# Two graph layers on one core: the products with counts in three passes, x in pieces, and layer 2's first operands fetched early

## The chip, the cores and the metric

The kernel runs on one core of one Trainium2 chip. The metric is the device time in microseconds of one execution on that core. A core has TensorE (PE, with its weight loads shown apart as PEld), VectorE (DVE), ScalarE (ACT), GpSimd (POOL) and SyncE (SP). Each engine takes its own instructions in the order in which they were written down; SP, ACT and POOL also issue DMAs in that order.

## The reference

A two-layer graph network (GIN) on 6250 nodes and 100000 edges, followed by a residual sum and a layer norm:

```
agg(h) = (1 + eps) * h + segment_sum(h[src], dst)
h1  = relu(relu(agg1(x) @ W1a + b1a) @ W1b + b1b)      # 256 -> 512 -> 512
y   = relu(agg2(h1) @ W2a + b2a) @ W2b + b2b           # 512 -> 512 -> 256
out = layernorm(x + y)
```

`x` is 6250 x 256 in float32. The edges are sorted by `dst`, and `dst` is 6250 times the square of a uniform number, so the first nodes have many edges and the last ones few: the first 768 nodes have about a third of all edges.

## The kernel before, in words

Nodes are taken in 49 tiles of 128, edges in 782 chunks of 128. The first tiles (six in layer 1, five in layer 2, the "heavy" ones, `HEAVY`) are summed in another way than the rest.

**Light nodes.** Chunks are taken in groups of four or more (`order`). For each chunk POOL issues one indirect DMA (L277) that gathers the 128 source rows into the buffer `early` (in layer 2 `early` and `late`); the buffers hold 24 chunks. PE adds the rows by slot with a 0/1 matrix (L1143), ACT copies the result (L1162), PE puts the slots in place (L1174), and DVE adds the result to the accumulators `acc` of the tiles concerned (L1166). Accumulators are seeded by a DMA on SP with the nodes' own rows (`seed`).

**Heavy nodes, layer 1.** For 264 chunks no rows are gathered. `counting` makes two 0/1 matrices for a chunk on DVE (`ca` at L965, `cb` at L968), PE multiplies them (L1011), ACT copies the sum (L1020) and DVE adds it into `at` (L981), a matrix of counts of source by destination in SBUF, that has room for four destination tiles (`RING`) at a time. It runs from the last chunk down, in 157 steps: the first 104 hold one chunk, then come 36 of two, 12 of four and 5 of eight. `turned_products` then multiplies: for each of 13 ranges of four source tiles (`RANGE`) it loads x (`load`), cuts it into three bf16 pieces whose sum is x (`pieces_of`, `thirds`: two casts on ACT, two subtractions on DVE), copies the counts to `ci` on ACT (L992), writes them to DRAM for layer 2 (`counts`), and PE multiplies pieces with counts (L917). This is done in two passes: tiles 4 and 5 (256 columns) while counting goes on, between steps 47 and 100, and tiles 0 to 3 (512 columns) after all counting. Each pass loads and cuts all of x.

**Heavy nodes, layer 2.** `products` loads each range of h1 and cuts it, loads the counts of one tile and range at a time (L864), and PE multiplies (L881) into one bank per tile and range; DVE adds that to `acc`.

**Dense part.** `block` takes two finished tiles: transposes (L772), the first product (L794), ReLU on ACT (L798), the second product (L808), and `finish`. Layer 1 writes h1 to DRAM from ACT's queue; layer 2 makes the layer norm and writes the output.

**Order.** All engines' instructions are written in one order (`manual_schedule`). After every chunk the program writes down one step of the dense blocks (`blockwise`, two blocks at a time) and as many steps of the heavy work (`beside`) as a credit allows. The credit per chunk (`spread`) is worked out from the estimated work of each kind; a step that costs nothing ends the turn. What evacuates a PSUM bank is written down 7 chunks later (`LAG`). At the end of a layer the rest is written out without gathers. Layer 2's gathers need all of h1, and before its first group six steps of `beside` are written.

Of the kernel before, what the change touches and what calls it, by code (L numbers as in the profile page):

```python
# [17 lines left out]
P = 128  # L18
# [134 lines left out]
def tile_gin_residual_layernorm(  # L153
# [359 lines left out]
    def weight(pool, w, kk, width, name):  # L513
        t = pool.tile([P, kk, width], F32, name=name)
        (nc.scalar if pool is const else nc.sync).dma_start(t, w.rearrange("(k p) f -> p k f", p=P))
        return t

    def second(pool):
        t = pool.tile([P, D], F32, name="b2b_s")
        nc.sync.dma_start(t, b2b.partition_broadcast(P))  # L520
        return weight(pool, w2a, KH, H, "w2a_s"), weight(pool, w2b, KH, D, "w2b_s"), t

    w1a_s = weight(const, w1a, KD, H, "w1a_s")
    w1b_s = weight(const, w1b, KH, H, "w1b_s")
# [39 lines left out]
    def ordered(ctx):  # L564
# [7 lines left out]
        counts = odram.tile([len(ranges), HEAVY[1], P, RANGE * P], F16, name="counts")  # L572

        def layer(number, ctx, table, width, scale, wa, ba, wb, wide, prepare, finish, conclude):
# [243 lines left out]
            UNIT = RANGE if number == 1 else RANGE // 2  # L818

            def load(r):  # L820

                units = []
                for u in range(0, len(ranges[r]), UNIT):
                    ks = ranges[r][u : u + UNIT]
                    xr = dense.tile([P, UNIT, width], F32, tag="xr", name="xr", bufs=2 if once else 3)
# [11 lines left out]
            def pieces_of(units):  # L837

                found = {}
                for ks, n, xr in units:  # L840
                    xp = dense.tile(
                        [P, 3, UNIT, width], BF16, tag="xp", name="xp", bufs=2 * RANGE // UNIT
                    )
                    if n:
                        thirds([xp[:, i, :n, :] for i in range(3)], xr[:, :n, :])
                    if n < len(ks):
                        m = rows(ks[n])
                        thirds([xp[:m, i, n, :] for i in range(3)], xr[:m, n, :])
                    for j, k in enumerate(ks):
                        found[k] = xp[: rows(k), :, j, :]  # L850
                return found

            def products():

                turns = [(r, t) for r in range(len(ranges)) for t in heavy]
                loaded, cut, factors = {}, {}, []

                def fetch(i):
                    r, t = turns[i]
# [649 lines left out]
```

## Time and profile before

| what | us |
|---|---|
| median of three runs | 1761.97 (1754.29 to 1763.14) |
| the profiled execution: its time | 1546.14 |
| the profiled execution: its span | 1544.2 |
| PE busy | 1315.8 (85%) |
| POOL busy | 1061.0 (69%) |
| DVE busy | 824.4 (53%) |
| ACT busy | 492.3 (32%) |

All durations are those of the profiled execution; its time and the median of the runs stand 216 us apart. The mean granted PE clock in it is 0.928. An engine's matmuls overlap and their ends are modelled, so a busy PE is not a PE at its peak; what one matmul takes is read from the starts of matmuls that follow each other. "issue" as a releaser means that the engine waited for nothing that the profile shows.

### The profile page before, as it was taken

How to read it: one execution, taken by the hardware profiler on the slowest of the kernel's cores; microseconds unless marked ns; L12 is line 12 of the kernel's file. 1: busy time of each engine (PE TensorE's matmuls, PEld its weight loads, DVE VectorE, ACT ScalarE, POOL GpSimd, SP SyncE). 2: the span in 40 equal slices, each digit the busy share in tenths (PEclk: the TensorE clock that was granted, in tenths of full speed). 3: DMA queues.
4: the chain of work that ended last, by engine and by line, in shares of the span. 5: the costliest groups of instructions: out<-in, count | busy, mean ns of one | idle time of the engine just before them, and what ended most of it. 6: DMA issues, size and time to landing. Idle time of an engine off the chain costs nothing.

```text
span 1544.2 us, 19261 instructions
## 1 busy us (share of the span) xinstructions
PE 1315.8 (85%) x6399; PEld 679.5 (44%) x6399; DVE 824.4 (53%) x2112; ACT 492.3 (32%) x897; POOL 1061.0 (69%) x1070
## 2 busy tenths in 40 slices
PE   2557778878888999999957798999999999999997
PEld 1114444434433444455522242444445655555556
DVE  7986666587763444333124335454545455556553
ACT  0455454342323444323332122222222222333131
POOL 6777777777777756773057777777777777777720
PEclk8668889998998999999978899999999999999999
DMA  5535654444435666543378888878888888888731
GB/s 144 155 98 147 183 174 147 131 134 126 135 115 170 193 185 205 149 136 97 105 243 284 271 282 259 280 245 282 257 281 260 259 260 248 261 265 251 236 115 34
DMA packets 144516, 301.14 MB, mean 195 GB/s; under 512 B 24430, under 2 KB 73242, under 8 KB 144408
## 3 DMA queue, kind: packets, MB, share of 16 engines
q0 software_dynamic: 67904, 209.00, 44.5%
q1 hardware_dynamic: 67196, 76.18, 15.1%
q10 hardware_dynamic: 9308, 14.64, 2.7%
q8 instruction: 54, 0.88, 0.2%
q14 instruction: 54, 0.44, 0.1%
HBM read 272.50 MB, written 27.23 MB: 194 GB/s over the span
## 4 chain that ended last, share of the span: by engine, by line
PE 55%; DMA 13%; DVE 12%; POOL 8%; issue 6%; ACT 5%; DVEq 1%; SPq 0%; ACTq 0%; POOLq 0%
PE bank L808 14%; PE bank L794 14%; PE bank L1143 8%; PE bank L1174 7%; PE bank L881 5%; POOL early L277 5%; PE bank L917 4%; DMA xr<-in_x_dram 3%; DMA early<-h,srcs 3%; POOL late L277 3%; DVE acc L1166 2%; DMA acc<-h 2%; DMA late<-h,srcs 2%; PE bank L1011 1%; PE bank L772 1%
## 5 line engine op out<-in xcount | busy, mean ns | idle before, releaser
L277 POOL DMA_INDIRECT early<-in_x_dram,srcs x518 | 525.7, 1015 | 184.7 <-issue 136.8
L277 POOL DMA_INDIRECT early<-h,srcs x274 | 267.5, 976 | 153.4 <-DMA h<-h1r 70.3
L1166 DVE SCALAR_TENSOR_TENSOR acc<-bank,mask,acc 128x256 f32<-128x256 f32 (+1 forms) x426 | 238.6, 608 | 232.3 <-PE bank L1174 178.9
L277 POOL DMA_INDIRECT late<-h,srcs x264 | 265.3, 1005 | 80.4 <-issue 64.0
L1143 PE MATMUL bank<-early,sel 128*32 128x256 f32 (+1 forms) x1584 | 167.1, 496 | 58.3 <-DMA early<-in_x_dram,srcs 32.8
L881 PE MATMUL bank<-xp,ci 128*128 128x512 bf16 (+1 forms) x735 | 177.7, 392 | 17.6 <-DMA ci<-counts 14.3
L794 PE MATMUL bank<-zt,w2a_s 128*128 128x256 f32 (+2 forms) x832 | 178.8, 369 | 4.9 <-ACT split L1162 2.0
L808 PE MATMUL bank<-w1b_s,ht 128*128 128x512 f32 (+1 forms) x392 | 180.8, 607 | 0.8 <-ACT ht L798 0.5
L1174 PE MATMUL bank<-split,to 128*128 128x256 f32 (+3 forms) x368 | 176.5, 563 | 3.1 <-DVE acc L1166 1.5
L794 PEld LDWEIGHTS bank<-zt,w2a_s 128*128 128x128 f32 x832 | 151.0, 191 | 43.4 <-issue 15.4
L881 PEld LDWEIGHTS <-ci 128*128 128x128 f16 (+1 forms) x735 | 71.7, 100 | 132.3 <-issue 62.8
L1162 ACT COPY split<-bank 128x256 f32<-128x256 f32 (+3 forms) x184 | 87.9, 483 | 130.1 <-PE bank L1143 101.1
L1011 PE MATMUL bank<-cb,ca 128*128 128x490 f16 x264 | 91.8, 416 | 43.7 <-DVE cb L968 14.5
L917 PE MATMUL bank<-ci,xp 128*128 128x256 f16 (+2 forms) x588 | 119.1, 348 | 5.9 <-ACT ci L992 5.9
L543 DVE TENSOR_TENSOR xr<-xr,xp 128x1024 f32<-128x1024 f32 (+2 forms) x51 | 60.2, 1181 | 106.9 <-ACT xp L542 95.7
L794 PE MATMUL bank<-zt,w1a_s 128*128 128x256 f32 (+1 forms) x400 | 102.4, 397 | 13.3 <-DVE acc L1166 5.6
L808 PEld LDWEIGHTS bank<-w1b_s,ht 128*128 128x128 f32 (+1 forms) x392 | 75.5, 196 | 85.1 <-issue 74.9
L1174 PEld LDWEIGHTS bank<-split,to 128*128 128x128 f32 (+1 forms) x368 | 58.1, 197 | 122.3 <-issue 76.2
L965 DVE TENSOR_SCALAR ca<-numbers,low 128x128 f16<-128x128 f16 x264 | 69.5, 263 | 72.1 <-PE bank L1011 71.7
L798 ACT ACTIVATE ht<-bank,b2a_s 128x256 f32<-128x256 f32 (+2 forms) x104 | 42.7, 460 | 183.7 <-PE bank L794 163.8
L1143 PEld LDWEIGHTS bank<-early,sel 128*32 128x32 f32 x1584 | 33.9, 112 | 149.2 <-issue 106.4
L1020 ACT CAST cs<-bank 128x490 f16<-128x490 f32 x157 | 85.6, 579 | 40.2 <-DVE at L981 28.1
(129 smaller groups left out, 1396.8 us busy)
## 6 DMA issues: line engine op xcount, KB each, us to landing
xr<-in_x_dram SPq DMA_DIRECT2D x24, 512.0 KB
h<-h1r ACTq DMA_DIRECT2D x48, 256.0 KB
xr<-h SPq DMA_DIRECT2D x24, 512.0 KB
acc<-h SPq DMA_DIRECT2D x23, 512.0 KB
early<-in_x_dram,srcs POOLq DMA_INDIRECT x518
ci<-counts SPq DMA_DIRECT2D x60, 128.0 KB
acc<-in_x_dram SPq DMA_DIRECT2D x24, 256.0 KB
counts<-ci SPq DMA_DIRECT2D x12, 512.0 KB
```

The costliest lines, as they stand in the source:

```text
L277: nc.gpsimd.indirect_dma_start(out=rows_[:, j, :], out_offset=None, in_=table, in_offset=bass.IndirectOffsetOnAxis(ap=srcs[:, c : c + 1], ...
L794: nc.tensor.matmul(ph[0][:, :nb], wa[:, k, f * P : (f + 1) * P], zt[:, k, :nb], start=(k == 0), stop=(k == kk - 1),)
L808: nc.tensor.matmul(po[0][:m], ht[:, f, i * P : i * P + m], wb[:, f, :], start=(f == 0), stop=(f == KH - 1),)
L881: nc.tensor.matmul(pm[0], ci[: rows(k), j * P : (j + 1) * P], cut[r][k][:, h, :], start=(j == 0 and h == 0), stop=(j == len(ks) - 1 and h ...
L917: nc.tensor.matmul(sums[f][0].rearrange("p (t c) -> p t c", c=P), cut[r][k][:, h, f * P : (f + 1) * P], factors[r][: rows(k), : len(ts), j ...
L965: nc.vector.tensor_scalar(a, numbers[:, :P], low[:, c : c + 1], None, op0=ALU.is_equal)
L1011: mm = nc.tensor.matmul(pc[0], a, b, start=(i == 0), stop=(i == n - 1))
L1020: nc.scalar.copy(cs, ap)
L1143: mm = nc.tensor.matmul(pm[0][b * SLOTS : (b + 1) * SLOTS], sel[:, c - c0, :], rows_[:, j, :], start=(c == parts[b][0]), stop=(c == parts[ ...
L1162: nc.scalar.copy(split[:used], ap[:used])
L1166: nc.vector.scalar_tensor_tensor(acc[t], ap, mask[:, t - lo[g], g : g + 1], acc[t], op0=ALU.mult, op1=ALU.add,)
L1174: nc.tensor.matmul(pu[0], to[:used], split[:used], start=True, stop=True)
```

## The change

- Layer 1 makes three passes of two tiles each (256 columns): tiles 4 and 5 as before; tiles 2 and 3 while the counting of tiles 0 and 1 goes on (from step 108, the products dealt over the steps after ten more); tiles 0 and 1 after all counting. The sums of a pass lie in one PSUM bank.
- Only the first pass loads and cuts x. It writes the pieces to DRAM (`x_cut`), and the other two load pieces from there, two ranges ahead. The last pass multiplies with `at` itself, without the copy `ci`.
- The counts for layer 2 go to DRAM as one tensor per range (`kept`), and layer 2 loads a range's counts in one DMA.
- The factor `ca` is made for four chunks in one DVE instruction.
- `at` and layer 2's rows, pieces and counts share one piece of SBUF (`room`). At the end of layer 1, when the heavy work is done and at most four groups are left, SP loads two ranges of h1 and one range of counts, and the first range is cut. Layer 2 takes ranges 2 to 12 first, then 0 and 1, and writes ten steps of `beside` before its first group. h1 is cut one tile at a time.
- `w1a_s` and `w1b_s` are no longer constants: they lie in a pool of layer 1, and layer 2's weights take their place.

```diff
+        kept = odram.tile([len(ranges), P, RANGE, LATE], F16, name="kept")
+        x_cut = odram.tile([len(ranges), P, 3, RANGE, D], BF16, name="x_cut")
...
+        line = [r for r in range(len(ranges)) if ranges[r][0] >= HEAVY[0]]
+        line += [r for r in range(len(ranges)) if r not in line]
...
             def products():
-                fetch(0)
                 yield 0.0
+                for i, t in [(i, t) for i in range(len(line)) for t in heavy]:
+                    r = line[i]
+                    if t == heavy[0]:
+                        fetch_counts(i + 1)
+                        fetch_rows(i + 2)
+                    if t == heavy[min(1, tiles - 1)]:
+                        cut_pair(i + 1, 0)
+                    if t == heavy[min(3, tiles - 1)]:
+                        cut_pair(i + 1, 1)
+                    ci = counts_of[i]
...
-            def turned_products(ts, factor):
+            def turned_products(ts, again, factor):
...
+                def come(r):
+                    if r < len(ranges):
+                        if again:
+                            xp = dense.tile(
+                                [P, 3, RANGE, width], BF16, tag="xp", name="xp", bufs=3
+                            )
+                            moved(r, xp, False)
+                            coming[r] = xp
+                        else:
+                            coming[r] = load(r)
 
                 def ready(r):
                     if r < len(ranges):
-                        cut[r] = pieces_of(loaded.pop(r))
+                        xp = coming.pop(r)
+                        if not again:
+                            xp = pieces_of(xp)
+                            moved(r, xp, True)
+                        found[r] = xp
                         factors[r] = factor(r, ts)
 
+                come(0)
+                come(1)
                 yield 0.0
                 ready(0)
-                sums = [place(n) for _ in range(kk)]
+                sums = place(kk * n, whole=True)
...
                         if j == len(ks) // 2:
                             ready(r + 1)
+                            come(r + 2)
...
-                        nc.vector.tensor_scalar(
-                            a, numbers[:, :P], low[:, c : c + 1], None, op0=ALU.is_equal
-                        )
+                            nc.vector.tensor_tensor(
+                                a, numbers[:, :P].unsqueeze(1).to_broadcast([P, AHEAD, P]),
+                                low[:, c0 : c0 + AHEAD].unsqueeze(2).to_broadcast([P, AHEAD, P]),
+                                op=ALU.is_equal,
+                            )
...
+                passes = [heavy[i : i + 2] for i in range(0, tiles, 2)][::-1]
+                for i, ts in enumerate(passes):
+                    first = END[ts[0]] + 1
+                    yield from advance(first)
+                    product = products_of(ts, i > 0)
+                    if ts[0] == RING:
+                        yield from along(product, apart)
+                        while cleared < len(ranges):
+                            yield 0.0
+                    elif ts[0] > RING:
+                        yield from product
+                    else:
+                        yield from along(product, len(STEPS))
...
             if number == 2:
-                for _ in range(6):
+                for _ in range(10):
                     beside.step()
...
+                if k >= len(order) - 4 and ahead and not beside.todo:
+                    ahead.pop(0)()
...
         with ExitStack() as inner:
-            layer(1, inner, x, D, e1[:, 0:1], w1a_s, b1a_s, w1b_s, H, prepare1, finish1, conclude1)
+            w1a_s, w1b_s = first_two(inner.enter_context(tc.tile_pool(name="first", bufs=1)))
+            ahead = [
+                lambda: (fetch_rows(0), fetch_counts(0)), lambda: fetch_rows(1),
+                lambda: None, lambda: cut_pair(0, 0), lambda: cut_pair(0, 1),
+            ]
```

`along(product, upto)` takes the counting steps up to `upto` and, after the first ten, deals the product's steps evenly among them. `fetch_rows` and `fetch_counts` issue SP's loads into `room`; `cut_pair` cuts two tiles of a range.

## The prediction

> **What bounds the kernel now.** I first cut the span by engine and stage. The columns are the stretch in us, its length, busy time of PE, of PE's weight loads, of DVE, ACT and POOL (with instruction counts), the granted PE clock, the DMA share and GB/s.
>
> ```profile
> 192.00:330.00 138.00, 114.44 (x596) 60.46 (x595) 93.31 (x283) 62.15 (x121) 105.74 (x106) 0.91 0.50 149
> 330.00:475.00 145.00, 116.82 (x566) 57.24 (x568) 98.69 (x336) 42.40 (x97) 111.48 (x111) 0.94 0.43 128
> 475.00:640.00 165.00, 152.44 (x697) 72.93 (x690) 64.94 (x113) 71.84 (x102) 111.95 (x111) 0.93 0.61 188
> 640.00:713.00 73.00, 69.99 (x340) 38.41 (x340) 31.29 (x75) 24.95 (x60) 55.56 (x58) 1.00 0.46 139
> 713.00:777.00 64.00, 59.84 (x211) 32.98 (x209) 13.69 (x27) 18.18 (x44) 0.69 (x1) 1.00 0.26 93
> 777.00:810.00 33.00, 18.73 (x76) 6.94 (x80) 8.62 (x7) 10.26 (x11) 20.27 (x20) 0.69 0.72 246
> ...
> 1220.00:1480.00 260.00, 249.67 (x1227) 149.98 (x1220) 143.14 (x307) 71.30 (x149) 197.22 (x207) 0.99 0.81 254
> ```
>
> POOL issues the gathers, one instruction each. It takes 145/111 = 1.31 us per gather while counting runs (330 to 475), 165/111 = 1.49 in 475 to 640, and 73/58 = 1.26 after that. So POOL paces layer 1 up to 475, something slows it from 475 to 640, and from 713 to 777 PE works alone. The waits by stretch (waiter, releaser, us in total, times, longest) tell what: the first line is from 330 to 475, the second from 475 to 640, the third from 640 to 777.
>
> ```profile
> PE bank L1143 <- DMA early<-in_x_dram,srcs: 14.4, 9, 2.9
> ...
> POOL early L277 <- PE bank L1143: 19.6, 9, 4.9
> ...
> POOL early L277 <- PE bank L1143: 3.1, 2, 2.8
> ```
>
> Before 475 PE waits for gathered rows and has 28 us idle. After it POOL waits for PE, 22.7 us in all. That is just where the products for four node tiles run: all 294 matmuls of 512 columns at L917 lie between 478 and 639. The timeline shows their pace (first line) and that of 256 columns (second), and then one dense block near the end of layer 1.
>
> ```profile
> 528.20 2.75 PE L917 MATMUL bank<-ci,xp 128*128 128x512 f16 x12
> ...
> 158.30 0.82 PE L917 MATMUL bank<-ci,xp 128*128 128x256 f16 x6
> ...
> 740.00 7.03 PE L808 MATMUL bank<-w1b_s,ht 128*128 128x512 f32 x16
> 746.87 3.62 PE L794 MATMUL bank<-zt,w1a_s 128*128 128x256 f32 x16
> ```
>
> Start to start, six of 256 take 0.66 us (the next instruction starts at 158.96), 0.110 each; the chain of waits gives twelve of 512 as 2.59 us, 0.216 each. A dense block of two tiles is 7.03 + 3.62 + 0.60 of transposes = 11.2 us of PE. At the layers' border:
>
> ```profile
> 783.95 0.94 POOL L277 DMA_INDIRECT early<-h,srcs  x1 [70.26 <-DMA h<-h1r]
> ...
> 789.34 0.58 PE L881 MATMUL bank<-xp,ci 128*128 128x512 bf16 x1 [14.30 <-DMA ci<-counts]
> ...
> 808.37 2.78 PE L1143 MATMUL bank<-early,sel 128*32 128x512 f32 x24
> ```
>
> POOL restarts only when the last row of h1 has landed. PE loses 15 us at its first products, and reaches the first group 25 us after POOL's restart, inside the 24 gathers that the buffers hold (24 x 1.29 = 31 us). POOL then issues 538 gathers by 1480.3, in 696 us, 1.29 each: it paces layer 2, followed by PE alone to 1544.
>
> **What the Trainium skill says.** "TensorE: Matmul & The Clock Gate", Back-to-back issue gap, gives 262 cycles for 256 columns and 518 for 512 at 2.4 GHz: 109 and 216 ns. The trace agrees (110 and 216), so narrower products cost nothing but their count. "SBUF — State Buffer", Who interferes with whom, says that a tensor_scalar in a two-port mode locks GpSimd out of the port it writes descriptors through, while tensor_tensor takes only reads. The trace agrees in sign: a gather's busy time is 1.004 us where counting runs, 0.958 where it has ended. "VectorE: DVE Perf Modes", The perf-mode tier table, gives tensor_tensor at most 2x on 16-bit data. "DMA: Bandwidth & Descriptors", Specifications, puts full rate at runs of 512 B or more; no wait in this trace shows short runs costing anything.
>
> **The change, part by part.**
> (1) Passes. Matmul work goes from 294 x 0.110 + 294 x 0.216 = 95.8 us to 882 x 0.110 = 97.0: +1.2 us. What counts is the place. Pass two (tiles 2 and 3) starts after counting step 108 + 10 and is dealt evenly over the 39 steps left; 22 of those hold two chunks, 12 four, 5 eight, so 56% of it falls on the first 44 of 132 chunks, which now run from about 285 us. Its 32.3 us thus go mostly where PE waited for POOL. The side queue's credit per gathered chunk is unchanged and so is its estimated work, so counting ends later, near 525 on the old clock, and pass three ends near the old 640. From 475 to 640 PE then has pass three (32.3), about a fifth of pass two (6) and some 40 chunks of counting (40 x 0.21 = 8.4), 47 in place of 63.5. PE's 152 falls to some 136, below POOL's 111 x 1.31 = 145. The stretch becomes POOL's: 165 to 145, of which I take **18** (bounds 8 and 22.7, the waits themselves).
> (2) PE's lag. POOL's last gather of layer 1 is issued at 712.7, PE's last gather sum starts at 724.4. With some 3 us to land, 8 are lag from the stretch before: take **7** (0 to 8).
> (3) The dense block of tiles 2 and 3 becomes ready near 535 instead of with tiles 0 and 1 after 640. The tail from 724 to 775 is 4.5 such blocks in a row; one goes from it: **11** (5 to 22). It lands in 535 to 640, in the room between PE's 136 and POOL's 145.
> (4) x pieces. The second cutting goes: 12 x (1.22 + 1.26) = 29.8 us of DVE, 12 x 2.09 = 25.1 of ACT. In cuts of 512 columns the first costs 24 x 2 x 0.68 = 32.6 of DVE (+2.8) and 24 x 2 x 0.59 = 28.2 of ACT (+3.1). ACT's copies of counts fall from 12 x (1.89 + 1.04) to 24 x 1.04, and pass three has none. For that SP issues 12 writes and 24 reads of 768 KB (27.6 MB) where 12 reads of 512 KB (6.3) were; the DMA share is 0.43 to 0.61 here, and the 21 MB are 0.05 of a share over 300 us. On SP a write waits for DVE's third piece; behind it stand the next load, the counts' write and seeds of accumulators, which are each issued one to two ranges early. Zero, covered by that lead. The first read of a pass has no lead: 768 KB at 1.5 times the old 5 to 6 us stands PE still for 8 to 9 us. Pass three replaces the old start (478.5 to 489.8, load, cut and copy); pass two's is new, covered by POOL's full buffers, +8 if they are not full.
> (5) First factors in fours: 264 x 0.263 = 69.5 us of DVE become 66 instructions of 128x512. Nearest row: the f32 is_equal of 128x512 at 0.683; at the tier table's 2x, an estimate, 0.41. So 27 to 45 us, and no longer two-port. Of the 0.046 us that a gather is longer, over some 300 gathers, 42% (69.5 of 69.5 + 95.4) is 6 us: take **3** (0 to 6).
> (6) Counts in one tensor per range: the same bytes, runs of 256 and 512 B written and 5 KB read. Zero; reads are off PE's path, being a range ahead. Layer 2's cuts per tile add 48 x 2 x 0.68 - 59.6 = 5.7 us of DVE and 6 of ACT, engines that idle half of that stage: zero.
> (7) Border. Two ranges and their counts are in SBUF, and the first range's pieces are cut, before the last h1 lands; their memory is last read by pass three, 100 us before. PE does five products at once and four more when the second range is cut. But w2a and w2b now take the memory of w1a and w1b, so SP holds their loads, and the accumulator seeds behind them, until the last L808 of layer 1 (they went at 762 to 764). Seeds, scaling and the second cut then end near 25 us after it, and PE gets to the first group 33 to 37 us after layer 1's last matmul; it was 33. POOL, which restarts 9 us after, blocks at about 40. Zero, and a few us of loss if that is missed. What is gained is 4 x 12 x 0.216 = 10.4 us of products done in PE's idle time. From 1220 to 1480 PE is busy 249.7 of 260 with no wait for rows, so part of that comes back at the end: **4** (-5 to 10).
> Sum: 18 + 7 + 11 + 3 + 4 - 1 = **42 us** off the profiled execution (span 1544.2, time 1546.1): 1504. The runs' median is 1762, 216 us above; no view shows where those lie. I carry the difference over unscaled: **1720**. Were every stage stretched alike, it would be 48 and 1714.
>
> **Rivals.**
> *POOL paces more than I think.* If the stretch to 640 is POOL's in the timed runs already (1056 gathers that took 0.2 us longer would make up the 216), items 1 and 2 are worth little and 3 with some of 7 remains: 15 us, 1747. For it: POOL's even pace; against it: its 22.7 us of waits on PE.
> *Late pieces: slower.* SP is one queue. A pass needs 13 loads; in pass three a range lasts about 6 us and the load is issued 1.5 ranges ahead, 9 us, against an estimated 7.5 to 10.8 us for 768 KB (1.5 times the 5.0 to 7.2 of the chain's xr loads), with seeds ahead of it in the queue. PE waits in order, the gather sums behind it, then POOL. From 42/26 = 1.6 us per load in both passes the gain is gone; at 2.5 it is +23, 1785. Against it: the old load had half a range of lead and a cut behind it, and cost 13 us in all.
> *Pass two overfills PE before 475.* PE's idle there is partly waiting for DVE's second factors, which more matmuls don't shorten. If 30 of the 32 us show as POOL waits, 10 us remain: 1755, no change.
> *The fetch comes too late to help*: item 7 falls to 0, 1724; inside my own range.
>
> **How the numbers follow.** Mine has 0.60, own range 1693 (69 off, all upper bounds) to 1749 (13 off). POOL's pace 0.15, overfilled 0.08, late pieces 0.17. Within 0.5% is 9 us, about what a measurement of this kernel can tell. Faster 0.75, same 0.08, slower 0.17. The range 1690 to 1770 leaves out most of the slow case and a few per cent below.
>
> **What would show it.** Right: no POOL wait on PE beyond 10 us from 285 to 640; layer 1's last gather near 690; four or fewer dense blocks after it; POOL's first gather from h1 at 740 to 750, and 696 us to its last; PE busy at the border. Wrong: PE waiting for the DMA of the pieces, POOL waiting on PE between 285 and 475, or the first group of layer 2 more than 40 us after the last L808. A tail of layer 1 still above 50 us breaks item 3.

## The result and the profile after

| kernel | median, us | lowest to highest |
|---|---|---|
| before | 1758.13 | 1753.57 to 1763.14 |
| after | 1778.11 | 1776.95 to 1782.20 |

The ratio is 1.0117, 95% interval 1.0078 to 1.0156: 20 us slower, where 42 us faster was forecast.

One thing has to be known before any trace is read. **The chips are of two sorts.** The kernel before takes 1754 to 1773 us on one sort and 1544 to 1546 us on the other. The profile that the prediction was made from (1546 us) is of the second sort, the runs shown beside it are of the first; for that profile this is told from its time and its trace alone. Each of the six chips of the later runs was used in one group only, so the chip and its state at that hour can't be told apart. So I compare only kernels run on the same chip, or traces of the same sort; "the slower sort" and "the faster sort" below mean this. The kernel after, run again on a chip of the faster sort, took 1557.42 us against 1546.35 (ratio 1.0060, 1.0035 to 1.0085). It is slower on both, so the chips don't excuse the forecast.

What differs between the sorts is read from the busy line (engine, us, share of the span, instructions) of the page of the kernel before on the slower sort, and of the kernel after on both, slower first:

```profile
PE 1397.1 (79%) x6369; PEld 700.3 (40%) x6399; DVE 830.6 (47%) x2112; ACT 492.0 (28%) x897; POOL 1063.4 (60%) x1070
```

```profile
PE 1407.4 (79%) x6693; PEld 728.3 (41%) x6693; DVE 805.5 (45%) x1960; ACT 467.4 (26%) x942; POOL 1035.2 (58%) x1070
```

```profile
PE 1317.2 (84%) x6661; PEld 708.0 (45%) x6693; DVE 803.7 (51%) x1960; ACT 467.3 (30%) x942; POOL 1037.8 (66%) x1070
```

DVE, ACT and POOL are busy for the same time on both sorts (DVE 824.4, ACT 492.3 and POOL 1061.0 in the profile before, against 830.6, 492.0 and 1063.4). So the instructions of these three are as fast, and what they lose lies between the instructions. PE's busy time, whose ends are modelled, is 81 to 90 us longer. What the change saves in work is there too: DVE 824 to 804, ACT 492 to 467.

The windows that answer to those of before, for the same gathers and on the same sort of chip (kernel after; us, busy us and instructions of PE, PEld, DVE, ACT, POOL, then clock, DMA share, GB/s):

```profile
182.00:349.00 167.00, 126.00 (x665) 68.57 (x665) 100.06 (x248) 70.87 (x140) 106.28 (x106) 0.87 0.57 177
349.00:493.00 144.00, 133.36 (x794) 75.58 (x792) 86.75 (x229) 52.29 (x108) 110.39 (x111) 0.99 0.63 196
493.00:638.00 145.00, 132.57 (x798) 80.41 (x796) 55.89 (x143) 33.16 (x80) 107.56 (x111) 0.96 0.70 224
638.00:711.00 73.00, 70.34 (x316) 36.99 (x316) 25.53 (x61) 21.30 (x53) 54.23 (x58) 1.00 0.54 171
711.00:778.00 67.00, 61.16 (x231) 33.42 (x232) 20.49 (x38) 22.64 (x51) 0.93 (x1) 1.00 0.19 63
778.00:810.00 32.00, 21.60 (x78) 8.11 (x78) 14.14 (x25) 11.99 (x19) 19.23 (x20) 0.79 0.85 318
1222.00:1488.00 266.00, 254.80 (x1257) 150.81 (x1257) 148.98 (x317) 77.03 (x159) 197.39 (x205) 0.99 0.80 246
```

Read against before, row by row: 138 us have become 167, 145 are 144, 165 are 145, 73 are 73, 64 are 67, 33 are 32, 260 are 266. The third row has the size that the prediction promised, 165 to 145 us, with PE busy 133 and POOL's pace of 1.31 us per gather; whether the third pass is the reason is asked below. In the second row, where pass two was put, PE is busy 133 us in place of 117 and the stretch is no longer. The first row ate the gain and more: 29 us for the same 106 gathers, with PE busy 126 of 167.

The following table has the whole kernel in that manner: us between the starts of POOL's gathers (L277), numbered from 0 to 1055; 517 is the last of layer 1, 518 the first of layer 2. "Both repairs" is a kernel of mine that is told of below. The columns are the traces before, f2, i1, b1 and after.

| gathers | before, faster sort | after | both repairs | before, slower sort | after |
|---|---|---|---|---|---|
| 0 to 111 | 150.4 | 144.5 | 146.1 | 174.4 | 166.9 |
| 111 to 185 (pass one) | 100.2 | 116.6 | 107.4 | 115.6 | 131.7 |
| 185 to 230 (its end) | 57.9 | 67.9 | 64.0 | 71.2 | 68.6 |
| 230 to 370 (pass two begins) | 184.0 | 184.3 | 184.3 | 205.4 | 209.5 |
| 370 to 444 | 114.8 | 93.0 | 94.0 | 128.5 | 120.3 |
| 444 to 517 | 96.1 | 96.9 | 93.4 | 110.7 | 112.1 |
| 517 to 518 (border) | 71.2 | 74.0 | 69.3 | 79.7 | 85.6 |
| 518 to 830 | 411.6 | 408.3 | 406.1 | 460.7 | 459.5 |
| 830 to 860 | 37.6 | 48.5 | 48.5 | 45.5 | 52.1 |
| 860 to 1055 | 246.2 | 246.7 | 246.7 | 290.5 | 286.2 |
| from 1055 to the end | 64.8 | 73.3 | 64.3 | 74.7 | 75.8 |

Single executions of one kernel lie up to 1% apart, so a row is believed when several kernels agree on it. Three losses pass that test, named here with the faster sort first: gathers 111 to 230, in which pass one lies (+26 and +13 us); the border, from the last gather of layer 1 to the first of layer 2 (+3 and +6); and gathers 830 to 860 (+11 and +7).

**Pass one.** The waits of the kernel before (faster sort, gathers 111 to 240; waiter, releaser, us in total, times, longest), and then those of the kernel after:

```profile
ACT acc L641 <- DMA acc<-in_x_dram: 6.9, 2, 4.2
ACT xp L542 <- DMA xr<-in_x_dram: 6.6, 3, 3.0
...
POOL early L277 <- PE bank L1143: 0.6, 2, 0.3
```

```profile
ACT xp L548 <- DMA xr<-in_x_dram: 26.7, 6, 6.4
POOL early L277 <- PE bank L1251: 26.5, 10, 9.1
...
ACT acc L709 <- DMA acc<-in_x_dram: 22.3, 3, 7.6
```

ACT stood 13.5 us for rows of x and for seeds before, and stands 49 us after. The chain goes on: the copies of the gathers' sums (`split`) stand behind that on ACT, PE waits for them, and POOL's wait on PE grows from 0.6 to 26.5 us, as much as the stretch is longer. In the kernel with both repairs it is 10.4 us:

```profile
POOL early L277 <- PE bank L1258: 10.4, 7, 4.7
```

**The border.** DMA issues of SP and ACT around the last store of h1, and POOL's first gather of layer 2, kernel after, faster sort (start, us, queue and line):

```profile
771.94 0.43 SPq L515 DMA_DIRECT2D w2a_s<-in_L_gnn_W2a_dram  x1
772.41 0.51 SPq L515 DMA_DIRECT2D w2b_s<-in_L_gnn_W2b_dram  x1
784.05 1.39 SPq L702 DMA_DIRECT2D acc<-h  x3
```

```profile
772.93 0.48 ACTq L1311 DMA_DIRECT2D h<-h1r  x1
```

```profile
784.98 1.00 POOL L277 DMA_INDIRECT early<-h,srcs  x1 [73.05 <-PE bank L934]
```

And SP and ACT in the kernel before:

```profile
762.69 0.43 SPq L515 DMA_DIRECT2D w2a_s<-in_L_gnn_W2a_dram  x1
763.16 0.51 SPq L515 DMA_DIRECT2D w2b_s<-in_L_gnn_W2b_dram  x1
763.71 2.11 SPq L634 DMA_DIRECT2D acc<-h  x3
```

```profile
776.46 0.48 ACTq L1199 DMA_DIRECT2D h<-h1r  x1
```

Before, w2's 1.5 MB were issued 14 us ahead of the last store (776.5). After, they wait for w1's memory and go out in the very microsecond ahead of it. From that store's issue to layer 2's first gather it took 7.5 us before, on both sorts, and 12.1 (faster) and 11.9 (slower) after. The DMA packets in the traces say how. On the slower sort the weights' queue moves 1.3 MB in the 4 us after 892.7, at some 330 GB/s, and the store's first packet comes 5.1 us after its issue (at 895.9), where it came 0.8 us after it before the change. From its first packet to the end of its last it then takes 5.5 us, against 5.4: the store isn't slowed, it starts later. POOL's gather follows the last packet by 1.3 us in both kernels, so it waits for the store, though the line above names PE, which gave the last signal.

What the early fetch was for did come true. The first products of layer 2 follow layer 1's last matmul without a pause, and then PE waits:

```profile
772.29 13.11 PE L934 MATMUL bank<-room 128*128 128x512 bf16 x58 [0.78 <-DVE h1r L1309]
792.90 3.67 PE L934 MATMUL bank<-room 128*128 128x512 bf16 x7 [7.50 <-DMA room<-kept]
...
810.93 1.50 PE L1251 MATMUL bank<-early,sel 128*32 128x512 f32 x12
```

The first group comes 25.9 us after POOL's restart; it was 24.4.

**Pace and blocks** have not changed. Six matmuls of 256 columns, and a dense block near the end of layer 1 (kernel after, faster sort):

```profile
562.50 0.82 PE L996 MATMUL bank<-room,xp 128*128 128x256 f16 x6
...
748.02 7.03 PE L876 MATMUL bank<-w1b_s,ht 128*128 128x512 f32 x16
754.89 3.62 PE L862 MATMUL bank<-zt,w1a_s 128*128 128x256 f32 x16
```

### The profile page after: what moved, and what is told of

It reads as the page before. It is cut to its first block, busy times and chain, and to the rows that moved or that the text cites. A ratio compares the mean times of both kernels' runs of the same rounds, so it can differ in the third digit from the quotient of the medians.

```text
span 1776.1 us, 19688 instructions
## 1 busy us (share of the span) xinstructions
PE 1407.4 (79%) x6693; PEld 728.3 (41%) x6693; DVE 805.5 (45%) x1960; ACT 467.4 (26%) x942; POOL 1035.2 (58%) x1070
## 4 chain that ended last, share of the span: by engine, by line
PE 48%; issue 17%; DVE 9%; another core or an unknown queue 8%; DMA 8%; ACT 4%; POOL 3%; SPq 1%; DVEq 1%; ACTq 0%; POOLq 0%
PE bank L862 11%; PE bank L876 10%; PE bank L1251 8%; PE bank L934 7%; PE bank L1282 5%; PE bank L996 3%; DMA acc<-h 3%; DMA xr<-in_x_dram 2%; PE bank L1075 2%; POOL early L277 2%; POOL late L277 1%; PE bank L840 1%; DVE acc L1274 1%; DVE room L1065 1%
## 5 line engine op out<-in xcount | busy, mean ns | idle before, releaser
L277 POOL DMA_INDIRECT early<-in_x_dram,srcs x518 | 514.4, 993 | 300.3 <-issue 133.9
L277 POOL DMA_INDIRECT early<-h,srcs x274 | 263.3, 961 | 224.0 <-PE bank L934 90.0
L1274 DVE SCALAR_TENSOR_TENSOR acc<-bank,mask,acc 128x256 f32<-128x256 f32 (+1 forms) x426 | 239.6, 609 | 256.2 <-PE bank L1282 73.7
L277 POOL DMA_INDIRECT late<-h,srcs x264 | 255.0, 966 | 141.2 <-issue 71.3
L1251 PE MATMUL bank<-early,sel 128*32 128x256 f32 (+1 forms) x1584 | 192.2, 535 | 68.9 <-ACT split L1270 35.6
L862 PE MATMUL bank<-zt,w2a_s 128*128 128x256 f32 (+2 forms) x832 | 192.5, 379 | 30.8 <-issue 23.2
L934 PE MATMUL bank<-room 128*128 128x512 bf16 (+1 forms) x735 | 185.4, 400 | 37.5 <-issue 17.6
L1282 PE MATMUL bank<-split,to 128*128 128x256 f32 (+3 forms) x368 | 184.3, 586 | 12.8 <-issue 6.9
L876 PE MATMUL bank<-w1b_s,ht 128*128 128x512 f32 (+1 forms) x392 | 183.5, 615 | 7.4 <-ACT ht L866 3.2
L1052 DVE TENSOR_SCALAR cb<-numbers,spot 128x490 f16<-128x490 f16 x264 | 90.0, 354 | 164.5 <-PE bank L1075 74.4
L934 PEld LDWEIGHTS <-room 128*128 128x128 f16 (+1 forms) x735 | 72.2, 101 | 154.1 <-issue 79.3
L996 PEld LDWEIGHTS <-xp 128*128 128x128 bf16 x882 | 91.7, 105 | 67.5 <-issue 44.1
L876 PEld LDWEIGHTS bank<-w1b_s,ht 128*128 128x128 f32 (+1 forms) x392 | 76.0, 198 | 92.1 <-issue 81.3
L1251 PE MATMUL bank<-late,sel 128*32 128x512 f32 x528 | 90.3, 651 | 27.2 <-issue 14.3
L996 PE MATMUL bank<-ci,xp 128*128 128x256 f16 (+1 forms) x588 | 91.7, 300 | 16.5 <-ACT ci L1109 11.3
L940 DVE TENSOR_TENSOR acc<-bank,acc 128x512 f32<-128x512 f32 x65 | 43.5, 683 | 132.8 <-remote 73.7
```

Source lines behind the costliest of these rows:

```text
L277: nc.gpsimd.indirect_dma_start(out=rows_[:, j, :], out_offset=None, in_=table, in_offset=bass.IndirectOffsetOnAxis(ap=srcs[:, c : c + 1], ...
L862: nc.tensor.matmul(ph[0][:, :nb], wa[:, k, f * P : (f + 1) * P], zt[:, k, :nb], start=(k == 0), stop=(k == kk - 1),)
L876: nc.tensor.matmul(po[0][:m], ht[:, f, i * P : i * P + m], wb[:, f, :], start=(f == 0), stop=(f == KH - 1),)
L934: nc.tensor.matmul(pm[0], ci[: rows(k), j, t * P : (t + 1) * P], cut[k][:, h, :], start=(j == 0 and h == 0), stop=(j == len(ks) - 1 and h ...
L940: nc.vector.tensor_tensor(acc[t], ap, acc[t], op=ALU.add)
L996: nc.tensor.matmul(sums[0][:, f * n : (f + 1) * n], found[r][:m, h, j, f * P : (f + 1) * P], factors[r][:m, j, :], start=(k == 0 and h == ...
```

## The experiments

My theory: the three passes give what the prediction said or less, and single new waits on SP's queue and on the DMAs take it away. The first rival: the schedule itself is at fault. Kernels in one group without another remark ran on one chip.

**The kernel before once more** (slower sort).

> The kernel before, unchanged. The profiled execution shown ahead of the prediction took 1546 us and the timed runs 1754 to 1763. If that execution was a fluke, this one takes about 1758, and its trace shows the stages as the timed runs have them: POOL held up by PE in layer 1, and POOL at 1.6 us per gather rather than 1.3. If profiled executions of this kernel are just faster, it takes about 1546 again.

Measured: 1768.25 us, beside 1773.36 for its twin. The 1546 us profile could not be had here. Later groups showed that it goes with the chip.

**`ca`, `x_cut`'s write, and the pieces through DRAM** (slower sort; before 1756.46, 44 runs).

```diff
 # c1: ca for one chunk at a time again
-                            nc.vector.tensor_tensor(a, numbers..., low[:, c0 : c0 + AHEAD]..., op=ALU.is_equal)
+                        nc.vector.tensor_scalar(a, numbers[:, :P], low[:, c : c + 1], None, op0=ALU.is_equal)
 # c2: every pass loads and cuts x; no x_cut
-                    product = products_of(ts, i > 0)
+                    product = products_of(ts, None)
 # c3: the write to x_cut five chunks later
-                            moved(r, xp, True)
+                            later(5, lambda: moved(r, xp, True))
 # c4: the kernel before, with ca in fours
```

> The kernel after, with ca made for one chunk at a time again (a 128x128 tensor_scalar on VectorE for each chunk in place of one 128x512 tensor_tensor for four). Theory A, that the three-pass schedule and what goes with it lose the time and ca in fours is a small gain: gather 111 of layer 1, which started 9 us earlier after than in the repeat of the kernel before, starts later again, and the time grows by 5 to 10 us, to 1783 to 1790. Theory B, that the 0.68 us instruction holds VectorE up at the head of hand-offs that TensorE waits for: the time falls by 10 to 20 us, to 1758 to 1768, and the 16 us lost between gathers 111 and 185 go.

Measured: 1778.46 us, ratio to before 1.0106 (1.0080 to 1.0131), against 1.0117 for the kernel after.

> The kernel before, with ca made for four chunks at once (the one part of the change done alone). Theory A: the 9 us by which the kernel after led at gather 111 came from this part, and the time falls by 5 to 10 us, to 1748 to 1753. Theory B (the 0.68 us instruction delays hand-offs): the time grows by 10 us or more, to 1768 or over.

Measured: 1754.08 us, 0.9990 (0.9967 to 1.0014). Both theories miss: `ca` in fours is worth nothing either way. The earlier start of gather 111 isn't its doing, for c1 has it too (167.7 us). Nor are gathers shorter: those of layer 1 are busy 1.016 us on average here, and 1.016 in the kernel before on the same sort.

> The kernel after, with the write of the pieces to x_cut issued five chunks later than the cut, so that it does not wait at the head of SP's queue. Theory A (the write holds up SP in pass one): gathers 111 to 185 take 10 to 16 us less, the time is 1762 to 1770. Theory B (the queue is not what pass one waits for): within 4 us of 1778, and the stretch from gather 111 to gather 185 stays at 130 us, against 115 in the repeat of the kernel before.

Measured: 1767.66 us, 1.0062 (1.0038 to 1.0087), 11 us less than c1, which on this chip stands for the kernel after. Gathers 111 to 185 took 123.7 us, against 131.7 after and 115.6 before: theory A in direction, with less than its 10 to 16 us.

> The kernel after, with x loaded and cut into three pieces afresh in each of the three passes; nothing is written to x_cut or read from it. Theory A, that the writes of x_cut stand at the head of SP's queue until their pieces are cut, and hold up the loads and seeds queued behind them: pass one gains about 16 us (gathers 111 to 185), passes two and three lose what 2 x 13 more cuts cost on ScalarE and VectorE (a cut of a range is 4 + 4 instructions of about 1 us, 26 x 4 us on each engine, a part of it on the path), in all 1765 to 1775. Theory B, that the passes through DRAM cost nothing and spare the cuts: slower than after, 1785 to 1800, with gathers 111 to 185 unchanged.

Measured: 1778.66 us, 1.0126 (1.0061 to 1.0191). Gathers 111 to 185 took 114.7 us, so with no traffic for `x_cut` the loss of pass one is all gone; but gathers 370 to 444 took 131.6. On the slower sort the pieces in DRAM do spare later passes time, and lose it again in pass one. Theory A had pass one right, and its total of 1765 to 1775 us was missed.

So the write costs, and half of its cost goes when it is moved. SP's own waits, kernel after, then c3 (160 to 320 and 160 to 300 us):

```profile
SPq L955 <- DVE xp L551: 206.0, 11, 104.9
```

```profile
SPq L1102 <- ACT ci L1109: 174.2, 8, 105.8
```

With the write out of the way SP's queue still stands, now for the copy of the counts, as it did in the kernel before (187.8 us in 10 waits). What c3 alters is the order: the load of x for the next range to be cut is issued ahead of the 768 KB write, not behind it. The traces of pass one show what that is worth. In every kernel the load of a range goes out only when the cut of the range before has ended, and its own cut waits for it, so that loads and cuts take turns. Averages over ranges 2 to 11, faster sort, in us:

| kernel | end of a cut to the next load | that load to its first cast | cut |
|---|---|---|---|
| before | 0.2 | 5.5 | 5.1 |
| after | 1.1 | 7.7 | 4.7 |
| both repairs (late write) | 0.85 | 6.6 | 5.0 |
| d4, told below (no write) | 0.9 | 6.1 | 5.1 |

The load's place in SP's queue changes by 0.2 us with the late write, and the time until its rows are used by 1.1. So what lies ahead of it on the DMAs counts for more than its place in the queue. On the slower sort the second column has 7.1 us after, 6.3 in c3 and 5.8 in c2; two runs of the old passes have 6.6 (b1) and 5.8 (c4), so it is less clear there.

**Border and passes** (faster sort; before 1545.77, 47 runs).

```diff
 # d1: the late write, and no early fetch: fetch and cuts begin with layer 2, 6 steps ahead of its first group
-            ahead = [lambda: (fetch_rows(0), fetch_counts(0)), ...]
+            ahead = []
 # e1: the late write, and w2's loads at layer 2's fourth group
+                if number == 2 and k == 3:
+                    bring()      # the three DMAs of second()
 # d3: the late write, and two passes
-                passes = [heavy[i : i + 2] for i in range(0, tiles, 2)][::-1]
+                passes = [heavy[RING:], heavy[:RING]]
 # d4: d3 and d1 and c2 at once
```

> The late write of x_cut, with the early fetch, and w2's loads issued at layer 2's fourth group in place of its beginning. Theory A, that w2's 1.6 MB stand before the last store of h1: the border falls from 85 to 88 us to 81, and the time by 4 to 6 us against the late write alone, to 1762 to 1764. Theory B, that the border is longer because the fetch and its cuts lie among the last dense blocks: the border stays, and the time is within 2 us of 1768.

Measured: 1537.85 us, 0.9950 (0.9928 to 0.9971). The border is 70.7 us, and store to gather 7.3: theory A for the border. Its 4 to 6 us in the whole time were said against the late write alone, which was not run on this sort.

> The late write of x_cut, and no early fetch: layer 2's first two ranges of h1, their counts and their cuts are issued when layer 2 begins, with 6 steps ahead of its first group. w1's place is still given to w2. Theory A, that the early fetch is what lengthens the border (last gather of layer 1 to first of layer 2, 85.6 us after, 79 to 80 before): the border falls back to 80 and the first 82 gathers of layer 2 take 2 or 3 us longer; 1764 against 1768 with the fetch. Theory B, that w2's 1.6 MB, which can only come when w1 has been read for the last time, hold up the last store of h1 (issued 11.9 us before layer 2's first gather after, 7.5 us before): the border stays at 84 or over, and the time grows to 1770, since only the small gain of the fetch is lost.

Measured: 1541.22 us, 0.9977 (0.9957 to 0.9997). Border 73.7 us, store to gather 11.7: without any fetch the last store is as late as with it. That, with e1, settles what delays the store: w2's transfer, not the fetch.

> The late write of x_cut, with two passes in place of three: tiles 4 and 5 among the counts, then tiles 0 to 3 in one pass after all counts, in two banks; all else as after. Theory A, that three passes gain what the traces of single executions say between gathers 333 and 517 (289 us after, 293 in the repeat of before): the time grows by 3 to 6 us against the late write alone, to 1771 to 1774. Theory B, that the schedule gives nothing because hand-offs, not TensorE's work, set the pace: within 3 us of 1768.

Measured: 1558.20 us, 1.0084 (1.0055 to 1.0112): 17 us behind d1, from which it differs in the passes and in the fetch, and 20 behind e1, from which it differs in the passes and in w2's loads. But the stretch that the third pass was made for is as short with two. Gathers 370 to 444 in the kernel before, in d3 and in e1 (columns as above):

```profile
501.90:616.70 114.80, 108.17 (x520) 52.90 (x519) 50.10 (x88) 54.28 (x76) 75.39 (x75) 0.96 0.63 195
507.70:601.70 94.00, 94.00 (x466) 46.46 (x465) 25.48 (x60) 18.69 (x44) 70.68 (x75) 1.00 0.79 246
507.10:601.80 94.70, 85.03 (x529) 53.00 (x528) 31.18 (x78) 19.52 (x46) 72.17 (x74) 0.96 0.77 248
```

With two passes PE is busy all the time and still keeps POOL's pace; the last gather of layer 1 comes at 698.1 us in d3 and 698.2 in e1. Of the 17 us the border has 9.5 (83.2 against 73.7). From the start of PE's last gather sum to that of its last second product (L876) d3 takes 58.0 us, d4, the next kernel, with two passes and no fetch 50.1, and d1 44.8. The fetch's cuts are in the way there: in d3's trace ACT makes eight casts of them from 708.3 to 716.3 us, the next copy `split` comes right behind, and PE waits for it.

```profile
716.59 1.22 PE L1284 MATMUL bank<-split,to 128*128 128x256 f32 x2 [5.75 <-ACT split L1272]
```

h1, told below, also has two passes and the fetch, and takes 58.6 us. No run takes the fetch alone away from d3.

> Two passes, x loaded and cut again in each, no x_cut, no early fetch: of the change only the new layout of the counts, ca in fours, layer 2's cuts of one tile at a time and w1's place being given to w2 are left. Theory A, that x_cut, the schedule and the border are all of the loss: 1760 (4 us of w2's collision at the border stay). Theory B, that layer 2's cuts or the layout of the counts cost too: 1768 or more, with layer 2 (gather 518 to 1055) longer than 797 us.

Measured: 1546.95 us, 1.0009 (0.9983 to 1.0034). As before in total, but not in its parts: gathers 370 to 444 take 99.5 us, not 114.8. So most of the gain in that stretch comes without a third pass and without pieces in DRAM, and in d3 nearly all of it without a third pass.

**After on the faster sort, and the order of ranges** (before 1546.35, 49 runs).

```diff
 # f1: e1, and layer 2's short range (one tile) last, as before the change
+        line.sort(key=lambda r: len(ranges[r]) < RANGE)
 # f4: e1 without early fetch, with layer 2's ranges in their old order
+        line = list(range(len(ranges)))
```

> The kernel after, unchanged. Theory A, that the sum of the prediction was wrong on any chip: slower than before by 0.5 to 1.3 per cent on this chip as well. Theory B, that the loss comes with the slower chips: where before takes about 1546 us, within 0.5 per cent of it. If before takes about 1760 us here, the ratio of 1.012 comes again and the question stays.

Measured: 1557.42 us, 1.0060 (1.0035 to 1.0085). Theory A.

> The late write and the late w2 with the change's own order of ranges, beside the others on one chip. From the traces so far it should be 4 us (the store of h1) and 8 to 16 us (the write of x_cut) below the kernel after, and 8 to 10 us above f1 if the order of the ranges makes the pile.

Measured: 1536.47 us, 0.9942 (0.9921 to 0.9964): two edits that change no arithmetic take 21 us off the kernel after.

> The late write and the late w2, and in layer 2 the range of one tile comes last, as in the kernel before, not third from the end. Theory A, that this order makes the pile of dense blocks at the end of layer 2's products: gathers 845 to 860 take 19 to 23 us in place of 29 to 35, and the time is 8 to 10 us below that of late write and late w2 with the change's order. Theory B, that the pile comes from the blocks of layer 2 all the same: no difference over 3 us.

Measured: 1539.45 us, 0.9961 (0.9943 to 0.9979). Gathers 845 to 860 fell from 29.2 to 18.9 us, as in the kernel before (18.8), and the time didn't fall: the stretch to gather 1055 grew from 246.7 to 249.5 and the end from 67.9 to 72.6, in traces of these two. The pile of dense blocks is made by the order of ranges, but it only moves PE's work about; layer 2's sum stays.

> The late write and the late w2, no early fetch, and layer 2's ranges in their old order 0 to 12. Theory A, as for f1: gathers 845 to 860 at 19 to 23 us; and the early fetch is worth 2 to 4 us, so 2 to 4 us slower than f1. Theory B, that the order of the ranges does nothing: 845 to 860 at 29 us or more.

Measured: 1539.91 us, 0.9969 (0.9953 to 0.9985); 18.9 us there too. The early fetch is worth 0.5 us against f1, which is nothing.

**Third pass, loads, cuts** (slower sort; before 1754.39, 42 runs).

```diff
 # h1: e1 with d3's two passes
 # h2: the kernel before, x loaded two ranges ahead in its passes
-                loaded = {0: load(0)}
+                loaded = {r: load(r) for r in range(2)}
...
                             ready(r + 1)
+                            if r + 2 < len(ranges):
+                                loaded[r + 2] = load(r + 2)
 # h2b: h2, x cut two tiles at a time
 # h3: c2 with e1's late w2
```

> The kernel before, with nothing changed but the loads of x in layer 1's passes, which are issued two ranges ahead of their use in place of one. Theory A, that ScalarE's waits for x (12.4 us in six waits between gathers 370 and 444, and 38.6 us of VectorE behind them) held the second pass up: gathers 370 to 444 fall from 115 to 100 to 105 us, and the time by 8 to 12 us, to 0.992 to 0.995 of before. Theory B, that the stretch is bound by TensorE's work as the prediction took it: within 3 us of before.

Measured: 1749.24 us, 0.9961 (0.9942 to 0.9980); gathers 370 to 444 in 122.2 us, against 128.5 and 128.8 in two runs without it: half of what theory A said. In that stretch the kernel before, in the profile on the faster sort, shows what is removed:

```profile
DVE xr L543 <- ACT xp L542: 38.6, 9, 7.3
POOL early L277 <- PE bank L1143: 19.6, 9, 4.9
...
ACT xp L542 <- DMA xr<-in_x_dram: 12.4, 6, 3.4
```

The second pass of the kernel before was held up in part by late rows of x, 12.4 us of them, and the prediction had read only POOL's line.

> The same, with x cut two tiles at a time (instructions of 512 elements) in place of four (1024), as the change does it. Theory A, that the shorter instructions let the hand-offs of the gathers through earlier: 3 to 6 us faster than h2. Theory B, that the loads are all of it: as h2, or slower by the fixed cost of twice as many instructions, up to 3 us.

Measured: 1754.10 us, 0.9995 (0.9971 to 1.0020). Short cuts give no gain over h2; this kernel is 5 us slower than h2, more than theory B's 3.

> The late write, the late w2 and the early fetch, with two passes (tiles 4 and 5, then 0 to 3) in place of three. Theory A, that the third pass is worth about what gathers 370 to 517 showed (two passes without x_cut 195.6 us there, three with it 188.7): 5 to 8 us slower than late write and late w2 with three passes (0.9942 to 0.995 of before), so 0.998 to 1.000. Theory B, that the prediction's 18 us belong to the third pass: 1.005 or more. Theory C, that the passes are worth nothing: 0.995.

Measured: 1752.22 us, 0.9986 (0.9959 to 1.0013). The number is theory A's, but the theories are set against a three-pass twin that has only been run on the faster sort, so the worth of the third pass in the whole time isn't measured on one chip. Gathers 370 to 444 took 114.8 us here, against 120.3 with three passes (c3), so two passes are no worse in that stretch on this sort either.

> The kernel after with the late w2, and x cut again in each of the three passes, nothing through DRAM. Theory A, that the detour through DRAM pays once its write is late: slower than late write and late w2 (0.9942 to 0.995) by 5 to 10 us, most of it between gathers 407 and 517. Theory B, that it does not pay: 0.995 or less.

Measured: 1784.33 us, 1.0163 (1.0122 to 1.0205). The ratio that it was to be set against is one of the faster sort. On its own sort it is slower than the late write (1.0062), as theory A has it, and not clearly slower than c2 (1.0126), which also cuts x in each pass. 134.2 us in gathers 370 to 444 (120.3 with the late write) show where.

**Both repairs a third time.**

> The late write and the late w2 with three passes, once more. Where the kernel before takes about 1755 us here: the late write alone stood at 1.0062 and the last store of h1 gains 4.5 us, so 1.0035 (1761 us) if the two add up; 0.995 if they do as on the faster chips. Against the two-pass twin at 0.9986 the first would mean that the third pass loses on such a chip. Where it takes about 1546 us: 0.995 again, and that stays open.

The chip was of the faster sort again: 1538.53 us against 1544.30, 0.9961 (0.9944 to 0.9978). So the late write and the late w2 make a kernel that beats both on the faster sort, in three groups of runs. On the slower sort it was not run; the late write alone stands at 1.0062 there, and the 4.5 us of the store would leave it at some 1.0036, so I don't claim it for that sort.

## Why the prediction was wrong, by its own steps

**Step 4, x's pieces: zero, "covered by that lead".** This is the step that failed most. It named the write, the load, the counts' write and the seeds in SP's queue, and let a lead of one to two ranges cover them. In the trace there is no such lead in pass one: a load goes out when the cut of the range before has ended, and its own cut waits for it, 5.5 us before the change and 7.7 after. Before the change this turn-taking cost POOL almost nothing (0.6 us of waits on PE's gather sums); with 768 KB to write per range it cost 26 us in gathers 111 to 230 on the faster sort and 13 on the slower. On the faster sort 13 of the 26 remain with the late write, and 6 without any write (d4). The rival "Late pieces: slower" had the right queue and the right sign and looked at passes two and three; for them the waits of the faster trace name a load of pieces once on PE, with 5.2 us. Where the pieces are written, not where they are read, it costs.

**Step 7, the border: a gain of 4.** It saw that w2 would wait for w1's memory, and asked only what would be late behind those loads: "Zero, and a few us of loss if that is missed". It did not ask what they would travel beside. The last store of h1, which POOL waits for, lands 4.5 us later, and the first group of layer 2 starts 39.4 us after the last L876 on the faster sort, where 33 to 37 was expected. As for the 10.4 us of products moved into PE's idle time: 58 matmuls of it do run there, but from gather 518 to the end the kernel after takes 776.7 us and the repaired one 765.7, against 760.2 before; d1, without the early fetch, takes 764.8. No profit from the early products is left at the end; why layer 2 gave more back than it got beyond the moved pile was not settled.

**Step 1, the passes: 18 us.** The size came out (165 us became 145 on the faster sort) and the reason did not, so the hit is luck. What was right is the place: gathers 230 to 370, among which pass two begins, take 184.3 us where they took 184.0, so its products did fit where PE waited. But for layer 1's gathers they needn't have been moved. With two passes gathers 370 to 444 fall from 114.8 to 94.0 us (d3), as with three (93.1 to 94.7 in d1, e1, f5 and i1); with two passes and x cut in both they fall to 99.5 (d4). So what shortens the stretch is among the edits that these kernels share with the change, such as the loads two ranges ahead, the shorter cuts and the last pass without `ci`. Of these only the loads were tried alone (h2, 6 us on the slower sort), and the rest stays open. The prediction read "POOL waits for PE" as too much work on PE, and did not follow PE's wait back to ACT and from there to a DMA. On the slower sort the stretch gained 8.2 us only.

**Steps 2 and 3, PE's lag and one dense block fewer: 7 and 11.** Taken from PE's last gather sum, the second products (L876) left over fell from 72 to 56, one block's sixteen, and the time to the last of them from 50.1 to 44.8 us: the block did go, for 5.3 us. But the lag from POOL's last gather to PE's last sum, which was to shrink by 7, grew from 11.6 to 15.2 us (20.1 to 25.6 on the slower sort). The two nearly cancel on the faster sort.

**Step 5, `ca` in fours: 3 us.** The instruction took 0.68 us, the upper bound: the double rate that the Trainium skill, "VectorE: DVE Perf Modes", The perf-mode tier table, allows for 16-bit data did not show with these broadcast operands. In time nothing came of it (c1, c4). The prediction had taken the longer gathers of the counting stage as a sign that `ca`'s tensor_scalar holds GpSimd up; without these 264 instructions (c4) the mean gather of layer 1 stayed at 1.016 us, so no run here shows it.

**Step 6: zero.** The tensors of counts gave no sign of a cost. The order of layer 2's ranges, which no step priced, made the pile at gathers 830 to 860 (+11 us), and undoing it gave nothing.

**The carry to the median** added the difference unscaled and said that no view showed where the 216 us lay. They go with the other sort of chip. The sign of the change is the same on both, so this did not turn the forecast. The parts did change: on the slower sort the gain in gathers 370 to 444 is 8 us and not 22, and the loss in 111 to 230 is 13 and not 26.

Of the signs listed, layer 1's last gather "near 690" was the decisive one: it came at 711 on the faster sort (before 712.7) and at 817 on the slower (815.4). POOL's waits on PE between 285 and 475, which were to show "pass two overfills PE", came to 12.6 us on the faster sort, so that rival was minor; the loss lay earlier, in pass one, where no sign had been set up.

## What to carry to other kernels

A lead is read off the queue, not off the program: here a load written down two ranges ahead went out only when the cut before it had ended, because what stood ahead of it in the queue waited for that cut. When a buffer's reuse moves a big load, ask which small transfer on the critical path it now meets: 1.5 MB, first used 118 us after layer 2's first gather (faster sort), delayed the store that this gather waited for. A wait of a pacing engine is followed back to the last link before it is called work: "POOL on PE" was in part "ACT on a load of x". And a gain of the forecast size doesn't prove its cause; a kernel that leaves the supposed cause out (d3) does test it.

## What the runs showed of the hardware

- Two sorts of chip ran one program 14% apart (1546 and 1756 us, medians of 49 and 44 runs), with busy times on DVE, ACT and POOL equal within 1%, and mean clocks in the profiles of the kernel before of 0.928 and 0.904. On the slower sort each of the ten traces has 93 to 120 waits that it can put down to no releaser, 409 to 553 us summed over the engines (POOL's longest in the kernel before 4.9 us); on the faster sort none of the ten has any. What the cause is was not found.
- A store of 212 KB issued on one queue a microsecond after 1.5 MB on another started late and then ran at its usual speed: its first packet came 4.9 to 5.1 us after its issue in the eight traces with w2's loads there, and 0.8 us in the twelve without, and from the first packet to the end of the last it took 5.3 to 5.7 and 5.4 us. From issue to the gather that waits for it that makes 11.4 to 12.1 us against 7.3 to 7.6, on both sorts of chip.
- VectorE's is_equal with both operands broadcast (tensor_tensor, 128x512, 16-bit in and out) took 0.68 us, as long as the f32 form.
